# Two states per recurrence instruction, norm constants off GpSimd, and a new order in a two-layer kernel

## The chip, the cores and the metric

The kernel runs on one core of a Trainium2 chip. Times are device microseconds (us); three runs were made, and their median is what is predicted. One more execution was profiled. The engines are called PE (matmuls; PEld is its weight load), DVE (VectorE), ACT (ScalarE), POOL (GpSimd) and SP, whose queue issues the DMAs.

## What is computed

Two layers over x of shape (2, 2048, 256), float32. In each, x becomes x + s(n) * silu(g(n)), where n is x normalised over its 256 columns.

```
layer 0: s = Mamba block, then FFN with gelu(tanh);  g = gated FFN with FP4-quantised inputs and weights
  step:  h = exp(dt_t * A) * h + dt_t * B_t * x_t     # h: (2, 512, 16), one t after the other
         y = sum over the 16 states of h * C_t
layer 1: s = attention over the two batch rows of each token (16 heads)
         g = three blocks: y = qlora(h); y = gelu(layernorm(y)); h = qlora(y) + h
```

The recurrence over t is the one sequential part: 512 channels, 16 states, 2048 steps, two batch rows. Its state starts at zero.

## The kernel before

**Tiles.** The 2048 positions are cut into NJ = 8 blocks of T = 256, for each of the two batch rows: 16 tiles, visited in the order (block, row). A tile passes through stages, one function each: head (line 864: two norms, input projection, convolution, dt, B and C, and ux = dt * xc), fp4_half (1013: quantise, gate and up products, quantise, down), scan (939: the recurrence, and the output projection with its sum x2), tail (1056: norm, FFN, gate, result x1). After both rows of a block, second (1100) does layer 1 for each half g of 128 positions, on streams s0 and s1; for the last block the streams are e0 and e1, which use tiles and PSUM banks that the finished work of layer 0 has left.

**The recurrence** (scan). Channels lie on partitions, in 4 groups m; time runs along the free dimension. For each of the 16 states n: ACT makes decay = exp(dt * A) by four activations into one of two decay tiles; DVE multiplies ux by B into hh; DVE runs a first-order scan over hh, all four groups in one instruction, each group led by one column (decay 0 there, hh the carried state); ACT copies the last columns to the tile state, for the next block; DVE multiplies hh by C, in place; PE transposes and adds the eight 128 x 128 pieces into two PSUM banks y. B and C of two states come by one broadcast DMA (bcs, two buffers). hh has four buffers, decay two; y2, the gated and transposed y, takes a fifth use of the hh buffers.

**Norms.** statistics (695) is DVE's bn_stats and bn_aggr. inverse_root (705) is two POOL instructions on [128, 2]: v * scale + plus, then the power -0.5. normalize (712) has DVE make -mean * root and ACT apply both. head calls inverse_root twice on the same variances. The norms in second's three blocks take the mean out of the weights instead: ACT squares with an accumulated sum, POOL makes the root, ACT scales.

**The order.** No instruction is issued where the code calls it. Recorder (line 32) records every call with its stage; prepare finds the dependences; forward (352) and backward (274) are list schedulers with a cost per instruction (cost, 104, and the tables SEEN and TAIL) that choose the order on each engine and the buffer of each tile; adjust and passes (1256 to 1280) are numbers that shift priorities of stages. issue (548) emits the chosen order, one queue per engine. So every instruction has the line of its emission, L561, in the profile, and is told apart by its tiles. [...]

Of the kernel before, what the change touches and what calls it, by code (L numbers as in the profile page):

```python
# [17 lines left out]
P = 128  # L18
# [23 lines left out]
class Recorder:  # L42
# [14 lines left out]
    TAIL = {"tensor": 0.165, "vector": 0.083, "scalar": 0.1, "gpsimd": 0.8, "sync": 1.7}  # L57
# [46 lines left out]
    def cost(self, engine, method, args, kwargs):  # L104
# [6 lines left out]
        if engine == "gpsimd":  # L111
            if method == "memset":
                return 0.04
            return 0.7 if method == "tensor_tensor" else 0.3
        values = list(args[1:]) + list(kwargs.values())
        tiles = [v for v in values if hasattr(v, "tensor") and v is not out]
        if engine == "tensor":
            rhs = args[2] if len(args) > 2 else kwargs.get("rhs")
            if method == "transpose" or kwargs.get("is_transpose"):
                return 0.109  # L120
            if rhs.dtype == BF16:
                return 0.1 + n / 2400.0
            lhs = kwargs.get("lhsT", args[1] if len(args) > 1 else None)
            if lhs.shape[0] == 16 and lhs.offset >= 16 * lhs.ap[0][0]:
                return 0.1
            return 0.005 + 4 * n / 2400.0
# [6 lines left out]
        if engine == "scalar":  # L133
            inside = bool(tiles) and self.space(tiles[0].tensor) == PSUM
            scalars += kwargs.get("accum_out") is not None
            return (0.05 if inside else 0.093) + 0.000833 * n + 0.1 * scalars
# [12 lines left out]
        if method in ("tensor_copy", "tensor_scalar", "memset") and n >= 64:  # L149
            return 0.07 + 0.00052 * n + 0.06 * scalars  # L150
# [50 lines left out]
    def prepare(self):  # L201
# [12 lines left out]
        for i, (engine, method, args, kwargs, stage) in enumerate(ops):  # L214
            if engine == "tensor":

                n = self.costs[i]
                lhs = kwargs.get("lhsT", args[1] if len(args) > 1 else None)
                if method == "transpose" or kwargs.get("is_transpose"):
                    self.size[i], self.table[i] = 128, 1  # L220
                elif lhs.dtype == BF16:
                    self.size[i], self.table[i] = (n - 0.1) * 2400, 2
                else:
                    self.size[i], self.table[i] = n * 2400 * lhs.shape[0] / 128, 3
            if engine == "sync":
                self.size[i] = 2 if args[0].dtype == BF16 else 4
                for d in args[0].shape:
                    self.size[i] *= d
# [28 lines left out]
    def order(self, lead, bonus, ahead, adjust=(), passes=()):  # L257
# [7 lines left out]
        for unit, bonus_back, ahead_back, bonus, ahead, adjust in passes:  # L265
            key = [-x / unit for x in self.backward(unit, bonus_back, ahead_back)]
            for b, k, v in adjust:
                for i, o in enumerate(self.ops):
                    if o[4] == (b, k):
                        key[i] += v  # L270
# [81 lines left out]
    def forward(self, key, bonus, ahead):  # L352
# [65 lines left out]
        while done < n:  # L418
# [28 lines left out]
            cost = costs[i]  # L447
            if best_e == "scalar" and table[i] and table[i] != now_table:
                t = max(t, free[best_e] + self.SWITCH)
                self.switched += self.SWITCH  # L450
                now_table = table[i]
# [113 lines left out]
def tile_two_layers(ctx: ExitStack, tc: tile.TileContext, a: dict):  # L565
# [25 lines left out]
    def t2k(stream, name):  # L591
        if stream == "e1":
            spare[0] += 1
            return mam.tile([P, 512], F32, tag=("dt", "ux", "lnt")[spare[0] % 3], name=name)
# [8 lines left out]
    power = const.tile([P, TG], F32, name="power")  # L603
    rec.gpsimd.memset(power, -0.5)

# [84 lines left out]
    decay = [const.tile([P, 4, T + 1], F32, tag=f"decay{i}", name=f"decay{i}") for i in range(2)]  # L690
    for t in decay:
        rec.gpsimd.memset(t[:, :, 0], 0.0)
# [12 lines left out]
    def inverse_root(stream, v, n, scale, plus, name):  # L705

        y = small.tile([P, n], F32, tag=f"ln_y_{stream.replace("e", "s")}", name=f"y_{name}")
        rec.gpsimd.tensor_scalar(y, v, scale, plus, ALU.mult, ALU.add)
        rec.gpsimd.tensor_tensor(y, y, power[:, :n], ALU.pow)
# [154 lines left out]
    def head(b, j, xt):  # L864
# [6 lines left out]
        rh = inverse_root("m", mv[:, :, 1], TG, 1.0 + EPS, EPS * EPS, f"a{nm}")  # L871
        normalize("m", xh, xt, TG, mv, rh, f"a{nm}")
        rx = inverse_root("m", mv[:, :, 1], TG, 1.0, EPS, f"x{nm}")
# [50 lines left out]
        ux = mam.tile([P, 4, T], F32, tag="ux", name=f"ux_{nm}")  # L924
        pdt = [bank("m", f"pdt_{nm}_{pr}").rearrange("p (m t) -> p m t", m=2) for pr in range(2)]
# [13 lines left out]
    def scan(b, j, h):  # L939
# [13 lines left out]
        for n in range(NS):  # L953
            if n % 2 == 0:
                bcs = scn.tile([P, 2, 2, T], F32, tag="bcs", name=f"bcs_{nm}_{n}", bufs=2)
                rec.sync.dma_start(bcs, bcv[:, n : n + 2, :].partition_broadcast(P))
            da = decay[n % 2]
            for m in range(4):
                rec.scalar.activation(
                    da[:, m, 1:], dt[:, m, :], AF.Exp, scale=amat[:, m, n : n + 1]  # L960
                )
            hh = scn.tile([P, 4, T + 1], F32, tag="hh", name=f"hh_{nm}_{n}", bufs=4)
            bn = bcs[:, 0, n % 2, :].unsqueeze(1).to_broadcast([P, 4, T])
            cn = bcs[:, 1, n % 2, :].unsqueeze(1).to_broadcast([P, 4, T])

            if j == 0:
                rec.gpsimd.memset(hh[:, :, 0], 0.0)
            else:
                rec.scalar.copy(hh[:, :, 0], state[b][:, n, :])
            rec.vector.tensor_tensor(hh[:, :, 1:], ux, bn, ALU.mult)  # L970
            flat = hh.rearrange("p m t -> p (m t)")
            rec.vector.tensor_tensor_scan(
                flat, da.rearrange("p m t -> p (m t)"), flat, 0.0, ALU.mult, ALU.add
            )
            if j < NJ - 1:
                rec.scalar.copy(state[b][:, n, :], hh[:, :, T])
            rec.vector.tensor_tensor(hh[:, :, 1:], hh[:, :, 1:], cn, ALU.mult)
            for g in range(TG):
                for m in range(4):
                    rec.tensor.matmul(  # L980
                        y[g][:, m * P : (m + 1) * P], lhsT=hh[:, m, 1 + g * P : 1 + (g + 1) * P],
                        rhs=ident, is_transpose=True, start=False, stop=(n == NS - 1),
                        skip_group_check=True,
                    )

        y2 = scn.tile([P, 4, T + 1], F32, tag="hh", name=f"y2_{nm}", bufs=4)[:, :, :T]
        for g in range(TG):
# [12 lines left out]
            rec.scalar.copy(y2[:, :, g * P : (g + 1) * P], pt)  # L1000
        po = bank("m", f"po_{nm}").rearrange("p (g d) -> p g d", g=TG)
        for g in range(TG):
            for m in range(4):
                rec.tensor.matmul(
                    po[:, g, :], lhsT=y2[:, m, g * P : (g + 1) * P],
                    rhs=w_out[:, m, :], start=(m == 0), stop=(m == 3),
                )
        x2 = mam.tile([P, TG, D], F32, tag="x2", name=f"x2_{nm}")
# [91 lines left out]
    def second(j, g, x1):  # L1100
# [3 lines left out]
        xv = x1[:, g, :, :]  # L1104
        xm = t2k(st, f"xm_{nm}").rearrange("p (b d) -> p b d", b=B)
        layer_norm(st, xm, xv, B, f"c{nm}")
# [66 lines left out]
        for k in range(3):  # L1173
# [11 lines left out]
            sq = small.tile([P, B], F32, tag=f"ln_sq_{st.replace("e", "s")}", name=f"sq_{nm}_{k}")  # L1185
            for bb in range(B):
                rec.scalar.activation(
                    yn[:, bb, :], py[:, bb, :], AF.Square, accum_out=sq[:, bb : bb + 1]
                )
            y = inverse_root(st, sq, B, 1.0 / D, EPS, f"f{nm}_{k}")  # L1190
            for bb in range(B):
                rec.scalar.activation(yn[:, bb, :], py[:, bb, :], AF.Copy, scale=y[:, bb : bb + 1])
# [15 lines left out]
            for m in range(2):  # L1208
                rec.scalar.activation(
# [23 lines left out]
    for i, (j, b) in enumerate(order):  # L1233
# [23 lines left out]
        (0, 0, 1.48), (0, 2, 0.93), (0, 3, -0.66), (1, 0, -1.29), (1, 1, -0.08), (1, 3, 0.49),  # L1257
        (1, 4, -0.55), (2, 0, -0.28), (2, 1, 0.62), (2, 4, 0.73), (3, 0, -0.1), (3, 4, 0.51),
        (4, 0, 0.15), (4, 1, 0.67), (4, 2, 0.59), (4, 3, -1.78), (4, 4, -0.74), (5, 0, -0.51),
        (5, 2, 0.63), (5, 3, 0.09), (5, 4, 0.29), (6, 0, 0.66), (6, 1, 1.68), (6, 2, 0.9),  # L1260
        (6, 3, 0.26), (6, 4, 2.72), (7, 0, 0.63), (7, 1, -0.41), (7, 2, 0.3), (7, 4, 0.34),
        (8, 0, -0.58), (8, 1, -0.58), (8, 2, 0.45), (8, 3, 0.6), (8, 4, -0.47), (9, 0, 0.76),
        (9, 1, 2.32), (9, 2, -0.12), (9, 4, -0.53), (10, 0, 0.19), (10, 3, 2.6), (10, 4, 0.12),
        (11, 0, 0.54), (11, 1, -0.16), (11, 2, -0.01), (11, 3, -0.3), (11, 4, 1.13),
        (12, 0, -0.62), (12, 1, 0.85), (12, 2, 0.08), (12, 4, 0.47), (13, 0, 0.34),
        (13, 1, -0.42), (13, 2, -1.48), (13, 4, -0.77), (14, 0, -1.31), (14, 1, 0.5),
        (14, 2, -1.21), (14, 3, -1.46), (14, 4, 0.39), (15, 1, 1.91), (15, 2, -0.55),
        (15, 3, 1.48), (15, 4, 0.61),
# [4 lines left out]
        (110, 0.3, 0.0, 0.5, 0.12, [(9, 0, 0.01)]),  # L1273
        (110, 0.3, 0.1, 0.5, 0.12, [(9, 0, 0.01)]),
        (80, 0.3, 0.0, 0.2, 0.12, []),
        (30, 0.3, 0.05, 0.5, 0.05, []),
        (20, 0.3, 0.1, 0.5, 0.12, []),
        (20, 0.3, 0.1, 0.5, 0.12, [(3, 4, 0.16)]),
    ]
    rec.issue(tc, lead=(0.28, -1.79, 0, -5.22, 1.4), bonus=366.531, ahead=0, adjust=adjust, passes=passes)  # L1280
# [48 lines left out]
```

## Time and profile before

| | us |
|---|---|
| median of three runs (1790.72 to 1791.84) | 1791.33 |
| the profiled execution | 1787.97 |
| its span, first to last instruction | 1786.2 |
| first and last recurrence instruction on DVE (tile hh), from the span's start | 49.9, 1675.1 |
| ACT table loads: 383 of 1283 ns | 491.4 |
| recurrence on DVE: 256 scans, 512 multiplies | 1197.3 |
| state copies on ACT, 448 of about 0.195 | 83.1 |
| POOL: 112 times scale and add, 112 powers | 229.5 |

In a group's row of the profile stand the engine, the operation, out<-in by the program's names, partitions x elements, the count, then the busy time and the mean ns of one, then the idle time of the engine just before and what ended it. "idle <-releaser" names the work whose end let the instruction go. Durations of one engine's neighbours overlap a little: a timeline, which lists start and duration, shows by how much. A float32 matmul of 256 columns stands as two records. The clock that TensorE was granted in the whole span was 0.947.

### The profile page before, as it was taken

The numbers are of one execution on the slowest core, as the hardware profiler recorded it, in microseconds if no ns is written. First come the engines' busy times: TensorE is split into PE (matmuls) and PEld (weight loads), VectorE is DVE, ScalarE is ACT, GpSimd is POOL, SyncE is SP. The second block draws the span as 40 slices with busy tenths as digits, with TensorE's granted clock in tenths as the row PEclk, the third lists the DMA queues.
The fourth block names the chain that finished last, engine by engine and source line by source line (L and its number), as shares of the span: only waits on it lengthen the run. The fifth ranks groups of instructions, "written<-read, shape, count | busy, mean of one in ns | idle before, by whom it ended". The sixth has DMA issues, their size and how long they took to land.

```text
span 1786.2 us, 22221 instructions
## 1 busy us (share of the span) xinstructions
PE 1585.8 (89%) x7756; PEld 1193.1 (67%) x7756; DVE 1630.4 (91%) x1926; ACT 1559.0 (87%) x3324; POOL 233.2 (13%) x265
## 2 busy tenths in 40 slices
PE   7448878999989989899998999999899999998887
PEld 5336656677776768676776767767676767766665
DVE  7999999999989999999998999999998999999711
ACT  7556968899988999989998999999999998999645
POOL 1000010022122201211111021101111102020101
PEclk9669989899999999999999999999999999999989
DMA  6311111111111111212121212211111111212000
GB/s 180 92 41 45 48 43 59 42 45 46 45 48 45 48 49 48 60 36 49 41 61 38 52 43 54 54 31 53 43 60 37 48 49 44 46 36 64 2 6 12
DMA packets 62989, 86.77 MB, mean 49 GB/s; under 512 B 15095, under 2 KB 29085, under 8 KB 62878
## 3 DMA queue, kind: packets, MB, share of 16 engines
q1 hardware_dynamic: 62878, 85.37, 17.9%
q8 instruction: 60, 0.98, 0.2%
q14 instruction: 51, 0.42, 0.1%
HBM read 80.62 MB, written 4.72 MB: 48 GB/s over the span
## 4 chain that ended last, share of the span: by engine, by line
ACT 41%; PE 32%; DVE 19%; issue 5%; POOL 2%; DMA 0%; ACTq 0%; DVEq 0%
ACT L561 14%; PE bank_f L561 13%; ACT decay L561 11%; DVE hh L561 10%; PE bank_m L561 7%; ACT t2k_s L561 6%; PE bank_s L561 5%; PE bank_y L561 4%; DVE fp_l L561 3%; ACT t2k_f L561 3%; PE bank_h L561 2%; POOL ln_y_s L561 2%; ACT xc L561 1%; DVE t2k_s L561 1%; DVE fp_sc L561 1%
## 5 line engine op out<-in xcount | busy, mean ns | idle before, releaser
L561 DVE TENSOR_TENSOR_SCAN hh<-decay,hh 128x1028 f32<-128x1028 f32 x256 | 581.4, 2286 | 5.7 <-ACT decay L561 4.4
L561 ACT ACT_TABLE_LOAD x383 | 491.4, 1283 | 13.9 <-DMA xt<-in_x_dram 3.7
L561 ACT ACTIVATE decay<-dt,amat 128x256 f32<-128x256 f32 x1024 | 445.0, 500 | 6.4 <-DVE hh L561 3.3
L561 PE MATMUL bank_y<-ident,hh 128*128 128x128 f32 x2048 | 296.5, 284 | 30.8 <-DVE hh L561 30.6
L561 DVE TENSOR_TENSOR hh<-hh,bcs 128x1024 f32<-128x1024 f32 x256 | 308.4, 1210 | 15.9 <-ACT state L561 15.2
L561 DVE TENSOR_TENSOR hh<-ux,bcs 128x1024 f32<-128x1024 f32 x256 | 307.5, 1210 | 1.7 <-PE bank_y L561 1.6
L561 PEld LDWEIGHTS bank_y<-ident,hh 128*128 128x128 f32 x2048 | 248.7, 146 | 82.3 <-DVE hh L561 43.1
L561 PE MATMUL bank_f<-w_f,t2k_f 128*128 128x256 f32 x512 | 133.7, 388 | 14.1 <-ACT t2k_f L561 14.0
L561 POOL TENSOR_SCALAR ln_y_s<-ln_sq_s 128x2 f32<-128x2 f32 x48 | 36.9, 769 | 769.8 <-ACT t2k_s L561 458.1
L561 PE MATMUL bank_m<-xi,cdiag 128*128 128x256 f32 x512 | 127.0, 380 | 0.0
L561 PE MATMUL bank_f<-t2k_f,w_f 128*128 128x256 f32 x512 | 124.6, 384 | 2.5 <-ACT t2k_f L561 2.5
L561 PEld LDWEIGHTS bank_f<-w_f,t2k_f 128*128 128x128 f32 x512 | 92.8, 192 | 36.0 <-ACT t2k_f L561 23.5
L561 PE MATMUL bank_f<-w_down,hq 128*128 128x256 f32 (+1 forms) x384 | 103.7, 409 | 7.3 <-ACT hq L561 7.2
L561 PEld LDWEIGHTS bank_f<-t2k_f,w_f 128*128 128x128 f32 x512 | 94.9, 190 | 21.0 <-ACT t2k_f L561 7.1
L561 PE MATMUL bank_h<-t2k_s,w_l 128*128 128x256 f32 x360 | 95.2, 399 | 9.5 <-ACT t2k_s L561 9.2
L561 PEld LDWEIGHTS bank_m<-xi,cdiag 128*128 128x128 f32 x512 | 93.0, 190 | 14.1 <-issue 0.7
L561 DVE SCALAR_TENSOR_TENSOR fp_l<-fp_h,fp_l 128x704 f32<-128x704 f32 (+2 forms) x124 | 91.4, 737 | 7.5 <-ACT fp_h L561 6.9
L561 PE MATMUL bank_f<-ident,fp_l 128*128 128x128 f32 x292 | 54.5, 311 | 47.1 <-DVE fp_l L561 46.5
L561 PE MATMUL bank_f<-w_gate,t2k_f 128*128 128x352 f32 x256 | 92.7, 481 | 2.2 <-ACT h L561 1.1
L561 PEld LDWEIGHTS bank_f<-w_down,hq 128*128 128x128 f32 (+1 forms) x384 | 71.8, 199 | 34.1 <-issue 12.7
L561 POOL TENSOR_TENSOR ln_y_s<-ln_y_s,power 128x2 f32<-128x2 f32 x64 | 93.2, 1457 | 5.2
L561 PE MATMUL bank_f<-w_up,t2k_f 128*128 128x352 f32 x256 | 90.2, 466 | 0.0
(187 smaller groups left out, 2589.9 us busy)
## 6 DMA issues: line engine op xcount, KB each, us to landing
bcs<-bc SPq DMA_DIRECT2D x128, 512.0 KB, 4.8
xt<-in_x_dram SPq DMA_DIRECT2D x16, 256.0 KB, 2.8
out_dram<-t2k_s SPq DMA_DIRECT2D x15, 256.0 KB, 3.8
w_f<-in_ffn_w_dram SPq DMA_DIRECT2D x2, 1024.0 KB
t2k_s<-in_qweights_dram SPq DMA_DIRECT2D x6, 256.0 KB, 2.9
w_in<-in_in_proj_w_dram SPq DMA_DIRECT2D x1, 1024.0 KB
h<-in_w_gate_dram SPq DMA_DIRECT2D x6, 128.0 KB, 2.1
w_qkv<-in_qkv_w_dram SPq DMA_DIRECT2D x1, 768.0 KB
```

Of the source, the lines that this page charges most:

```text
L561: getattr(getattr(self.nc, engine), method)(*args, **kwargs)
```

## The change

It does six things.

- **Two states per call.** hh, decay and the multiplies take two states: [128, 2, 4, 257]. One multiply by B, one scan (2056 elements), one multiply by C, one state copy in and out for a pair. hh has two such buffers, decay two (twice the bytes). The activations and PE's transposes keep their number and size.
- **Room for it.** ux and x2 have one buffer instead of two. y2 is no longer an hh buffer: its two halves take turns on the one buffer t2k_m that head's xh uses too.
- **Norm constants.** v * scale + plus is a DVE instruction now; POOL keeps the power. head makes both constants side by side and one power of four columns. In second's blocks ACT makes it (Identity with scale 1/256 and a bias tile eps).
- **The last block's tiles** (streams e0, e1): normalising is done by DVE (subtract, multiply); the blocks' norms use bn_stats and one DVE multiply instead of ACT's square, sum and scaling; half of hn goes to DVE. The spare tiles of e1 are dt, dt, lnt.
- **The planner**: costs and latencies of POOL, of small matmuls, of accumulating activations and of DVE reading PSUM; a POOL instruction that isn't a memset is planned only where DVE is free; priorities may be shifted for one engine of a stage.
- **adjust, passes, lead, bonus, ahead** are other numbers, so the order on every engine is another.

Counted in the built programs: DVE 1928 to 1650 instructions (branches among them), ACT 3230 to 3006, POOL 270 to 127, PE and SP the same number; ACT table loads 383 to 373.

```diff
@@ Recorder
-    TAIL = {... "gpsimd": 0.8, ...}
+    TAIL = {... "gpsimd": 0.3, ...}
...
+            if best_e == "gpsimd" and table[i]:
+                t = max(t, free["vector"])
@@ inverse_root
-        y = small.tile([P, n], ...)
-        rec.gpsimd.tensor_scalar(y, v, scale, plus, ALU.mult, ALU.add)
-        rec.gpsimd.tensor_tensor(y, y, power[:, :n], ALU.pow)
+        m = 2 * n if and_also else n
+        y = small.tile([P, m], ...)
+        rec.vector.tensor_scalar(y[:, :n], v, scale, plus, ALU.mult, ALU.add)
+        if and_also:
+            rec.vector.tensor_scalar(y[:, n:], v, *and_also, ALU.mult, ALU.add)
+        rec.gpsimd.tensor_tensor(y, y, power[:, :m], ALU.pow)
@@ head
-        ux = mam.tile([P, 4, T], F32, tag="ux", name=f"ux_{nm}")
+        ux = mam.tile([P, 4, T], F32, tag="ux", name=f"ux_{nm}", bufs=1)
@@ scan
-        for n in range(NS):
-            if n % 2 == 0:
-                bcs = ...; rec.sync.dma_start(bcs, ...)
-            da = decay[n % 2]
-            for m in range(4):
-                rec.scalar.activation(da[:, m, 1:], dt[:, m, :], AF.Exp, scale=amat[:, m, n : n + 1])
-            hh = scn.tile([P, 4, T + 1], F32, tag="hh", name=f"hh_{nm}_{n}", bufs=4)
+        for n in range(0, NS, 2):
+            bcs = ...; rec.sync.dma_start(bcs, ...)
+            da = decay[n // 2 % 2]
+            for k in range(2):
+                for m in range(4):
+                    rec.scalar.activation(
+                        da[:, k, m, 1:], dt[:, m, :], AF.Exp, scale=amat[:, m, n + k : n + k + 1]
+                    )
+            hh = scn.tile([P, 2, 4, T + 1], F32, tag="hh", name=f"hh_{nm}_{n}", bufs=2)
...
-                rec.scalar.copy(hh[:, :, 0], state[b][:, n, :])
-            rec.vector.tensor_tensor(hh[:, :, 1:], ux, bn, ALU.mult)
-            flat = hh.rearrange("p m t -> p (m t)")
+                rec.scalar.copy(hh[:, :, :, 0], state[b][:, n : n + 2, :])
+            rec.vector.tensor_tensor(hh[:, :, :, 1:], un, bn, ALU.mult)
+            flat = hh.rearrange("p k m t -> p (k m t)")
...
-                rec.scalar.copy(state[b][:, n, :], hh[:, :, T])
-            rec.vector.tensor_tensor(hh[:, :, 1:], hh[:, :, 1:], cn, ALU.mult)
+                rec.scalar.copy(state[b][:, n : n + 2, :], hh[:, :, :, T])
+            rec.vector.tensor_tensor(hh[:, :, :, 1:], hh[:, :, :, 1:], cn, ALU.mult)
...
-        y2 = scn.tile([P, 4, T + 1], F32, tag="hh", name=f"y2_{nm}", bufs=4)[:, :, :T]
+            y2[g] = t2k("m", f"y2_{nm}_{g}").rearrange("p (m t) -> p m t", m=4)
...
-        x2 = mam.tile([P, TG, D], F32, tag="x2", name=f"x2_{nm}")
+        x2 = mam.tile([P, TG, D], F32, tag="x2", name=f"x2_{nm}", bufs=1)
@@ second
+        last = st[0] == "e"
...
+            if last:
+                mv = statistics(st, py, B, f"f{nm}_{k}")
+                y = inverse_root(st, mv[:, :, 1], B, 1.0, EPS, f"f{nm}_{k}")
+                rec.vector.tensor_tensor(yn, py, y.unsqueeze(2).to_broadcast([P, B, D]), ALU.mult)
+            else:
...
+                rec.scalar.activation(sq, sq, AF.Identity, scale=1.0 / D, bias=eps)
+                rec.gpsimd.tensor_tensor(y, y, power[:, :B], ALU.pow)
...
+                if last and m == 1 and k < 2:
+                    rec.vector.tensor_scalar(hn[:, m, :], hb[:, m, :], wt["odd"][:, k, m : m + 1], None, ALU.add)
+                    continue
@@ adjust, passes, issue
-    rec.issue(tc, lead=(0.28, -1.79, 0, -5.22, 1.4), bonus=366.531, ahead=0, ...)
+    rec.issue(tc, lead=(12.22, -6.26, 0, -7.42, 1.15), bonus=193.318, ahead=0.034, ...)
```

## The prediction

> **What bounds the kernel now.** I read the page's first part, then busy time by stretch, then VectorE's waits, then the groups, then timelines.
>
> The first part shows three engines near 90%, so it decides nothing:
>
> ```profile
> PE 1585.8 (89%) x7756; PEld 1193.1 (67%) x7756; DVE 1630.4 (91%) x1926; ACT 1559.0 (87%) x3324; POOL 233.2 (13%) x265
> ```
>
> I cut the span at VectorE's first and last recurrence instruction (those on tile hh), at 49.9 and 1675.1 us. Columns: stretch, length, busy us (instructions) of PE, PEld, DVE, ACT, POOL, then clock, DMA.
>
> ```profile
> 0.00:49.90 49.90, 39.56 (x180) 29.30 (x181) 35.90 (x121) 35.88 (x70) 8.88 (x25) 1.00 0.69 178
> 49.90:1675.10 1625.20, 1452.79 (x7173) 1097.07 (x7173) 1569.92 (x1750) 1463.53 (x3123) 213.65 (x218) 0.95 0.18 47
> 1675.10:1786.20 111.10, 93.47 (x407) 66.72 (x405) 24.59 (x57) 59.57 (x132) 10.67 (x23) 0.93 0.02 8
> ```
>
> In the middle DVE works 1569.9 of 1625.2 us and is idle 55.3: it is the bound there. In the last 111 us it is nearly empty: a chain PE-ACT-DVE-POOL sets that end. DVE's longest waits in the middle:
>
> ```profile
> DVE hh L561 <- ACT state L561: 15.2, 14, 3.5
> DVE sz L561 <- PE bank_y L561: 7.4, 6, 4.3
> DVE hh L561 <- ACT decay L561: 4.4, 6, 1.8
> ```
>
> The groups, and DVE's timeline for what one instruction really occupies:
>
> ```profile
> L561 DVE TENSOR_TENSOR_SCAN hh<-decay,hh 128x1028 f32<-128x1028 f32 x256 | 581.4, 2286 | 5.7 <-ACT decay L561 4.4
> L561 DVE TENSOR_TENSOR hh<-hh,bcs 128x1024 f32<-128x1024 f32 x256 | 308.4, 1210 | 15.9 <-ACT state L561 15.2
> L561 DVE TENSOR_TENSOR hh<-ux,bcs 128x1024 f32<-128x1024 f32 x256 | 307.5, 1210 | 1.7 <-PE bank_y L561 1.6
> ```
>
> ```profile
> 905.63 1.22 DVE L561 TENSOR_TENSOR hh<-hh,bcs 128x1024 f32<-128x1024 f32 x1
> 906.77 1.22 DVE L561 TENSOR_TENSOR hh<-ux,bcs 128x1024 f32<-128x1024 f32 x1
> 907.91 0.68 DVE L561 TENSOR_TENSOR fp_l<-fp_l,fp_sc 128x512 f32<-128x512 f32 x1
> 908.51 1.22 DVE L561 TENSOR_TENSOR hh<-ux,bcs 128x1024 f32<-128x1024 f32 x1
> ```
>
> A multiply lasts 1.22 us but the next starts 1.14 us on; the 512-element one takes 0.60. So an element costs (1.14-0.60)/512 = 1.05 ns and the instruction 0.06 to 0.07 us. Two scans take 4.41 us from start to next start in the same timeline (898.91 to 903.32): 2.205 each, of which 1028 elements at twice that rate leave again some 0.065.
>
> **The change, middle stretch.**
>
> *Pairs.* 768 recurrence instructions become 384 of double length: 384 fixed parts go, 384 x 0.067 = **-25.7 us**. [...] I take 25.7. No row shows a multiply over two states with both operands broadcast; if the longer pattern streams no faster than two instructions do, the gain is 0; if not even that, the kernel loses; the nearest rows scale by elements, so I keep the full gain.
>
> *Constants of the norms.* 70 two-element DVE instructions replace GpSimd ones, 55 of them in the middle. The nearest row (ln_m, two elements) lasts 0.146; in the timeline two take 0.22 with the second's tail, so 0.075 each: **+4.1**. The 42 of the LoRA norms go to ACT instead, 0.1 each on an engine that doesn't bound.
>
> *Moved by the new order.* I counted the built orders. Before the first hh instruction stand 148 DVE instructions instead of 122 (two more weight blocks quantised, one more LoRA weight, less one ux): **-5.4** from the middle. After the last stand 121 instead of 57; of the work that was in the middle, one quantisation of 704 columns (4.4), the two gate products (0.9), one attention mix (2.6) and a gate by s (1.2) are now behind: **-9.1**.
>
> Sum: 1569.9-25.7+4.1-5.4-9.1 = 1533.8 of work. Idle 55.3 kept: **1589**, against 1625.
>
> Does the idle stay? For it: decay now holds four states instead of two, so ACT may run further ahead; state copies fall by 224 (0.08 us from start to start at 920.03, so 18 us of ACT), table loads from 383 to 373 (1.30 each: 13). Against it: hh holds the same bytes in two pieces, not four. In the orders, DVE has 3.4 us of other work on average between a scan and the multiply by C, which waits for ACT's state copy; in the new one 2.6. And ux, x2 have one buffer, y2 shares one. The ux product now has to stand between the last multiply by B of one tile and the first of the next; all three are on DVE, and only ACT's dt can be late (0.2 us now): 0, at worst 1 us in each of 14 tiles. The second y2 copy waits for four matmuls on the first, about 1.7 us; PE has other work (bank_f, bank_s); 0, at worst 16 x 1.7. I take 55, and 30 to 85 for the range.
>
> *GpSimd.* One instruction per norm instead of two. Power takes longest beside DVE:
>
> ```profile
> L561 POOL TENSOR_TENSOR ln_y_s<-ln_y_s,power 128x2 f32<-128x2 f32 x64 | 93.2, 1457 | 5.2
> 1673.03 3.06 POOL L561 TENSOR_TENSOR ln_y_s<-ln_y_s,power 128x2 f32<-128x2 f32 x1
> 1741.99 0.69 POOL L561 TENSOR_TENSOR ln_y_s<-ln_y_s,power 128x2 f32<-128x2 f32 x1
> ```
>
> 0.69 beside an idle DVE, 3.06 beside a busy one. [...] by the row that hardly matters, since DVE waits for GpSimd only 2.4 us in the whole middle, ACT 13.1. As one of two such waits goes, I take 0, and +3 for the range.
>
> **First stretch.** x is now the eleventh DMA on SP's queue instead of the first: 7 small issues of 0.3 and 3 of 0.5 us ahead, +4 us for the first head. But the bias rows' DMAs, which held the queue from 30.9 to 34.5 and the broadcast of B and C behind them, stand earlier. DVE's 36+5 us of work fit. I take **50**, unchanged (46 to 55).
>
> **End stretch**, by its landmarks in the timelines: last hh ends 1675.1; x2 at 1691.1; the FFN's sum 1714.0; second's transposed input 1725.0; end 1786.2.
> - x2: in the new order all of the last quantisation and eight gate/up products stand ahead of it on DVE. A 256-column matmul takes 0.44 us (the chain has 56 records, two each, in 12.41 us). 11.4 us of DVE work, transposes and copy 1.1, six w_down 2.7, eight of 352 columns 4.9, Silu and product 1.1, quantisation with its trip to ACT 6: 27 instead of 16, **+11**.
> - FFN: 11 more matmuls of the previous tile interleaved on PE, 0.44 each: **+5**.
> - second's norm: before, ln_m waited behind two other DVE instructions until 1721.7, then ACT made four halves in 2.1 us. Now four DVE instructions of 0.2 follow the power directly: **-4**.
> - three blocks per tile: the squares took ACT 0.84, statistics take DVE 0.97; GpSimd 0.96 becomes 0.69; scaling 0.82 becomes 0.69; the two halves of hn run side by side, 0.84 to 0.47. Some 0.7 to 1 each, **-3**. ACT no longer serves both tiles in turn, and the second tile, which ends last and lagged by 10 us (1731.5 against 1741.2), has its q, k, v ahead of the first one's output product: **-4**.
>
> 111+5 = **116** (106 to 124).
>
> **Sum.** 50+1589+116 = 1755 of span; 1.8 lie around it (1787.97-1786.2), and the median of the runs is 3.4 above that execution: **1760**.
>
> **Rivals.**
> 1. As worked out, 1760: 0.62.
> 2. The deeper decay buffers and the lighter ACT take half of DVE's idle: 1760-28 = 1732. For: 19.6 of the 55 us are waits for state and decay. Against: no engine gets slack, PE's work is unchanged. 0.16.
> 3. The end gives the gain back: +16 for its longer chain and none of the 11 saved: 1771; with y2's wait uncovered half the time (+13), 1784. 0.14.
> 4. Slower: the multiply by C stalls in place. In the new order 50 of 128 scans have under 1.5 us of other DVE work before it (40 of 256 before). ACT's queue puts a table load and an activation, 1.3+0.5, ahead of the copy. If each of these lost one load, 50 x 1.28 = 64, less the 15 paid now: +49, 1809. It decides from 0.6 us per tight pair on. Against: the last tiles need no copy, and loads became fewer. 0.05.
> 5. The pair instructions stream slower than by elements: at 2% more, +22, 1782; 0.03.
>
> A measurement can tell 0.2%, 3.6 us, from no change. Faster (below 1787.7): 0.62+0.16+0.12+0.02 = 0.92; within: 0.03; slower: 0.05. The range takes in idle of 30 (1735) and, upward, rival 3's 1784.
>
> **What would show it.** Scan near 4.43 us and multiply near 2.28 by duration, or the pairs are priced wrong. DVE busy 1530 to 1540 between first and last hh, idle near 55; if "DVE hh <- ACT state" exceeds 40, rival 4 acts. ux, x2, y2 must not appear as long waits. x2 some 27 us after the last hh. Wrong if PE, whose matmuls it doesn't change, turns out to hold the middle at 1625: then DVE's idle would simply grow by 36.

## The result and the profile after

The changed kernel took 1790.03 us (median of 20 runs, 1783.87 to 1792.72), the kernel before 1791.12 on the same chips (20 runs): a ratio of 1.0000, 95% interval 0.9987 to 1.0012. The prediction, 1760, is missed by 30 us; the time did not change. The profiled execution of the changed kernel took 1792.72, its span is 1790.5. It lies 2.7 us above its median, the profiled one of the kernel before 3.2 below its own: differences of a few us between the two profiles mean nothing.

The first part of the page:

```profile
PE 1591.0 (89%) x7756; PEld 1206.1 (67%) x7756; DVE 1622.9 (91%) x1648; ACT 1519.2 (85%) x3088; POOL 164.2 (9%) x122
```

Busy time by stretch, cut as before at the first and last hh instruction of DVE (now 63.5 and 1668.9):

```profile
0.00:63.50 63.50, 45.62 (x167) 32.83 (x168) 42.51 (x147) 32.44 (x70) 4.16 (x15) 0.87 0.61 161
63.50:1668.90 1605.40, 1440.32 (x7110) 1097.48 (x7110) 1532.21 (x1382) 1428.94 (x2910) 151.50 (x95) 0.95 0.18 47
1668.90:1790.50 121.60, 105.02 (x482) 75.80 (x480) 48.19 (x120) 57.81 (x109) 8.52 (x12) 0.99 0.02 7
```

DVE's work in the middle is 1532.2 us; 1533.8 was predicted. What was not predicted is its idle time: 73.2 instead of 55. The middle is 1605.4 (predicted 1589), the first stretch 63.5 (50), the end 121.6 (116). Against the kernel before, the middle became 19.8 us shorter, but the first stretch 13.6 longer and the end 10.5.

DVE's longest waits in the middle:

```profile
DVE hh L567 <- ACT state L567: 19.2, 26, 3.8
DVE hh L567 <- PE bank_y L567: 14.7, 7, 5.0
DVE h L567 <- PE bank_f L567: 11.2, 10, 3.3
```

The second and third stood at 1.6 and 2.0 before. The groups of the recurrence:

```profile
L567 DVE TENSOR_TENSOR_SCAN hh<-decay,hh 128x2056 f32<-128x2056 f32 x128 | 567.0, 4429 | 1.5 <-ACT hh L567 0.7
L567 DVE TENSOR_TENSOR hh<-hh,bcs 128x2048 f32<-128x2048 f32 x128 | 291.6, 2280 | 19.7 <-ACT state L567 19.2
L567 DVE TENSOR_TENSOR hh<-ux,bcs 128x2048 f32<-128x2048 f32 x128 | 291.5, 2277 | 14.9 <-PE bank_y L567 14.7
```

Scan 4.43 and multiply 2.28, as priced; two single ones took 2 x 2.286 and 2 x 1.210 before.

The prediction left out part 4 of the page, the chain that ended last. It goes back from the last instruction, at each step to what released it or to the instruction before it on its engine, and gives each engine's share of the span. Before:

```profile
ACT 41%; PE 32%; DVE 19%; issue 5%; POOL 2%; DMA 0%; ACTq 0%; DVEq 0%
```

After:

```profile
PE 41%; ACT 40%; DVE 13%; issue 5%; POOL 1%; DMA 0%; ACTq 0%; DVEq 0%
```

DVE, busiest of all in the middle, stood on a fifth of the chain before the change. The two kernels' progress agrees in the long run, though their orders differ everywhere. Starts of the multiply by B of some pairs, in us:

| pair (of 128) | 1st | 5th | 17th | 73rd | 113th | last |
|---|---|---|---|---|---|---|
| before | 49.9 | 106.3 | 251.0 | 959.2 | 1476.1 | 1665.1 |
| after | 63.5 | 108.0 | 251.7 | 958.7 | 1476.4 | 1657.7 |

Between these pairs they differ more, either way: at the 13th the changed kernel is 10.1 us behind, at the 22nd 10.2, at the 42nd 20.0 ahead, at the 103rd 15.7 behind. Over pairs 5 to 128 it is 1.2 us behind on average. So the late start is made up by about the 33rd pair, and after that little is gained before the last tile. This suggests that something that the change left alone sets the pace.

### The profile page after: what moved, and what is told of

Read it like the earlier page. It is cut to its first block, busy times and chain, and to the rows that moved or that the text cites. A ratio compares the mean times of both kernels' runs of the same rounds, so it can differ in the third digit from the quotient of the medians.

```text
span 1790.5 us, 21456 instructions
## 1 busy us (share of the span) xinstructions
PE 1591.0 (89%) x7756; PEld 1206.1 (67%) x7756; DVE 1622.9 (91%) x1648; ACT 1519.2 (85%) x3088; POOL 164.2 (9%) x122
## 4 chain that ended last, share of the span: by engine, by line
PE 41%; ACT 40%; DVE 13%; issue 5%; POOL 1%; DMA 0%; ACTq 0%; DVEq 0%
PE bank_f L567 15%; ACT L567 14%; ACT decay L567 11%; PE bank_m L567 10%; DVE hh L567 8%; PE bank_s L567 7%; PE bank_y L567 6%; ACT t2k_s L567 5%; PE bank_h L567 3%; DVE fp_l L567 3%; ACT t2k_f L567 3%; ACT xc L567 1%; ACT dt L567 1%; POOL ln_sq_s L567 1%; ACT fp_h L567 1%
## 5 line engine op out<-in xcount | busy, mean ns | idle before, releaser
L567 DVE TENSOR_TENSOR_SCAN hh<-decay,hh 128x2056 f32<-128x2056 f32 x128 | 567.0, 4429 | 1.5 <-ACT hh L567 0.7
L567 ACT ACT_TABLE_LOAD x373 | 478.6, 1283 | 15.2 <-PE bank_h L567 4.1
L567 PE MATMUL bank_y<-ident,hh 128*128 128x128 f32 x2048 | 283.2, 286 | 31.2 <-DVE hh L567 31.2
L567 DVE TENSOR_TENSOR hh<-hh,bcs 128x2048 f32<-128x2048 f32 x128 | 291.6, 2280 | 19.7 <-ACT state L567 19.2
L567 DVE TENSOR_TENSOR hh<-ux,bcs 128x2048 f32<-128x2048 f32 x128 | 291.5, 2277 | 14.9 <-PE bank_y L567 14.7
L567 PE MATMUL bank_f<-w_f,t2k_f 128*128 128x256 f32 x512 | 134.0, 392 | 17.0 <-ACT t2k_f L567 16.9
L567 POOL TENSOR_TENSOR ln_sq_s<-ln_sq_s,power 128x2 f32<-128x2 f32 x42 | 74.4, 1771 | 742.7 <-ACT ln_sq_s L567 742.7
L567 PE MATMUL bank_f<-w_up,t2k_f 128*128 128x352 f32 x256 | 91.2, 473 | 10.1 <-ACT h L567 6.4
L567 PE MATMUL bank_f<-w_gate,t2k_f 128*128 128x352 f32 x256 | 91.9, 480 | 2.7 <-ACT h L567 1.9
L567 PE MATMUL bank_s<-w_l,t2k_s 128*128 128x256 f32 x336 | 87.0, 395 | 7.4 <-ACT t2k_s L567 7.3
```

The lines of the kernel that those rows point to most:

```text
L567: getattr(getattr(self.nc, engine), method)(*args, **kwargs)
```

## The experiments

My theory after the result: ScalarE's and TensorE's queues pace the middle, and time taken from DVE turns into idle time. Its first rival: DVE does pace it, and the pairs' coarser pieces cost as much by waits as they save. All kernels but three (order_free, free_state, and bcs_early, which moves two DMAs) keep the planned order of the kernel that they start from and change instructions only where issue emits them; of(v) is the name of v's tile. Measured, all in one table (each ratio is to the kernel before on the same chip; the last column is (ratio - 1) x 1791):

| run | median us | ratio, 95% interval | us |
|---|---|---|---|
| (the change itself) | 1790.03 | 1.0000, 0.9987 to 1.0012 | 0 |
| split | 1788.51 | 0.9990, 0.9979 to 1.0001 | -2 |
| dve_pad | 1786.81 | 0.9966, 0.9952 to 0.9979 | -6 |
| dve_cut | 1785.71 | 0.9954, 0.9940 to 0.9968 | -8 |
| before_cut | 1771.90 | 0.9903, 0.9876 to 0.9930 | -17 |
| half_transposes | 1796.18 | 1.0032, 1.0020 to 1.0045 | +6 |
| pe_pad | 1804.97 | 1.0083, 1.0055 to 1.0112 | +15 |
| act_pad | 1811.88 | 1.0115, 1.0085 to 1.0146 | +21 |
| act_half | 1768.87 | 0.9864, 0.9839 to 0.9890 | -24 |
| pe_act_cut | 1758.73 | 0.9794, 0.9771 to 0.9816 | -37 |
| rest_cut | 1733.45 | 0.9683, 0.9658 to 0.9709 | -57 |
| no_power | 1780.64 | 0.9931, 0.9910 to 0.9952 | -12 |
| shift_c | 1797.75 | 1.0041, 1.0027 to 1.0055 | +7 |
| bcs_early | 1792.05 | 1.0003, 0.9992 to 1.0014 | +1 |
| order_free | 1785.07 | 0.9941, 0.9922 to 0.9959 | -11 |
| state_dve | 1774.06 | 0.9876, 0.9856 to 0.9897 | -22 |
| more_dve | 1788.49 | 0.9970, 0.9948 to 0.9992 | -5 |
| free_state | 1775.99 | 0.9905, 0.9890 to 0.9920 | -17 |
| before_state | 1804.63 | 1.0070, 1.0056 to 1.0083 | +12 |

**Is VectorE the bound?** Four kernels: the pairs undone, VectorE loaded, and relieved, after and before the change.

split:

```diff
+    if engine == "vector" and of(args[0]) == "hh":
+        for k in range(2):      # half k of every operand
+            cut = slice(k * 4 * (T + 1), (k + 1) * 4 * (T + 1)) if method == "tensor_tensor_scan" else k
+            emit(engine, method, [v[:, cut] for v in operands])
```

> The changed kernel's order kept instruction for instruction, but each of the 384 recurrence instructions over two states issued as two over one state, back to back. Theory A (VectorE sets the middle and the pairs save their fixed parts): 384 x 0.067 = 25.7 us more, about 1816, the idle time of VectorE between first and last hh stays near 73. Theory B (the middle is held by other engines and queues, the saved time turns into idle): the split is absorbed, 1790 to 1800, and VectorE's idle falls to about 50.

The middle of split (stretch, length, busy us of PE, PEld, DVE, ACT, POOL):

```profile
61.30:1663.60 1602.30, 1438.87 (x7109) 1092.43 (x7108) 1551.79 (x1766) 1429.66 (x2910) 126.13 (x95) 0.95 0.18 47
```

DVE works 19.6 us more than in the changed kernel, and the middle is 3.1 shorter: idle 50.5 instead of 73.2. That is theory B of that text. So the pairs' saving is real work saved (for a multiply 0.068 per pair: two single ones follow each other at 1.135, a pair at 2.202), and undoing it cost no time. But the shorter pieces also helped others: in the middle the powers on GpSimd took 124.5 us instead of 149.9, and TensorE's idle time before the matmuls into y, until hh was ready, fell from 31.2 to 20.2. So this result alone would also fit the rival, VectorE's cost hidden by waits saved.

dve_pad:

```diff
+    if engine == "vector" and of(args[0]) == "hh":
+        nc.vector.memset(spare, 0.0)      # spare: [128, 16]
```

> The changed kernel's order kept, and behind each of the 384 recurrence instructions a memset of 16 columns on VectorE, some 0.065 us each: the same 25 us of VectorE's time that the split cost, without its shorter pieces. Theory A (VectorE is only 13% of the chain that ended last, ScalarE and TensorE hold the middle): 3 to 6 us more, 1793 to 1796. Theory B (VectorE does set the middle, and the split was free because its shorter pieces release TensorE and ScalarE earlier): 20 us more or over, 1810.

Not more but 6 us less. As a load it failed: the memsets, 384 of 0.072 us, lie mostly in the tail of the instruction before (one starts at 1121.39, where the multiply before it ends at 1121.44), and DVE's busy time in the middle grew by only 6.4. So it cannot decide against theory B. A place where it gained stands below, at GpSimd.

dve_cut, and before_cut with the same edit on the kernel before:

```diff
+    if engine == "vector" and method == "tensor_tensor" and of(args[1]) == "hh":
+        seen += 1
+        if seen % 2: continue
```

> The changed kernel's order kept, but the multiply by C is left out for every second pair (64 x 2.20 = 141 us of VectorE less); the output is then not the reference's. Theory A (VectorE does not set the middle): 13% of it, some 18 us, 1765 to 1785. Theory B (VectorE sets it): 70 us less or more, until the next engine holds at about 1720.

> The kernel before with its own order, but the multiply by C left out for every second state (128 x 1.14 = 146 us of VectorE less); the output is not the reference's. Theory A (VectorE did not set the middle before the change either, 19% of the chain): 10 to 28 us less than the kernel before, 1763 to 1781. Theory B (it did, and only the changed order moved the bound): 60 us less or more, 1730.

The middle of dve_cut, then of before_cut:

```profile
62.50:1658.30 1595.80, 1437.77 (x7102) 1097.14 (x7101) 1397.54 (x1318) 1428.40 (x2909) 140.13 (x95) 0.94 0.19 47
50.00:1656.00 1606.00, 1443.63 (x7167) 1092.39 (x7166) 1436.66 (x1622) 1460.92 (x3122) 186.58 (x218) 0.95 0.18 48
```

DVE has 134.7 us less to do and the middle loses 9.6; DVE is idle for 198 us. In before_cut 133 us less give 17. The outcome is nearest theory A both times (dve_cut even gained less than the 18 us named there): a us taken from DVE was worth 0.13 before the change, where the chain gave it 19%, and 0.06 after it. This refutes the first half of the rival: if DVE paced, the cuts would have shown it. That the coarser pieces cost something by waits is not refuted; split's waits say that they do, and how much is open.

**What paces the middle?** Loads and cuts on the other two.

act_pad and pe_pad:

```diff
+    if args[2] == AF.Exp and args[0].shape[-1] == T:  # act_pad
+        exps += 1
+        if exps % 4 == 0: nc.scalar.copy(spare, power)      # four elements
...
+    if engine == "tensor" and method == "transpose":  # pe_pad
+        turns += 1
+        if turns % 4 == 0: nc.tensor.transpose(*args, **kwargs)      # once more
```

> The changed kernel's order kept, and behind every fourth decay exponential a copy of four elements on ScalarE: 256 x 0.09 = 23 us more of ScalarE's time. Theory A (TensorE sets the pace; leaving out 226 us of ScalarE's work took only 21 off): 2 to 6 us more. Theory B (ScalarE, with 40% of the chain that ended last, sets it as much as TensorE): 10 us more or over.

> The changed kernel's order kept, and every fourth plain transpose issued twice: 217 more matmuls of about 0.11 us, 24 us more of TensorE's time, nothing else changed. Theory A (TensorE's queue sets the pace of the middle): 15 to 25 us more, 1805 to 1815. Theory B (no single engine does, each has slack of its own): under 8 us more.

The middle of act_pad, then of pe_pad:

```profile
64.10:1687.30 1623.20, 1442.53 (x7109) 1093.58 (x7108) 1533.20 (x1382) 1451.10 (x3162) 152.37 (x95) 0.95 0.18 47
64.50:1683.80 1619.30, 1455.65 (x7300) 1116.91 (x7299) 1532.89 (x1382) 1432.18 (x2910) 156.49 (x95) 0.95 0.18 47
```

22 us more of ScalarE make the middle 18 longer and the time 21: 0.9 us for each. TensorE's 19 us more in the whole span (15.3 in the middle) cost 15: 0.8 for each, theory A at its lower end. ScalarE's outcome is theory B of its text: a load on it is paid as much as one on TensorE. On VectorE split's 19.6 us cost nothing. What speaks against waits saved by shorter pieces as the reason is state_dve below: it adds 17 us to VectorE with the pairs whole and gains 22; had the 17 been paid in full, the 19 us taken off ScalarE would have to be worth twice their size. It does not settle it, as that move also ends VectorE's waits for the copies (19.2 us).

act_half and half_transposes, and pe_act_cut with both edits:

```diff
+    if args[2] == AF.Exp and args[0].offset >= 4 * (T + 1):  # act_half: the pair's second state
+        exps += 1
+        if exps > 8: continue
...
+    if engine == "tensor" and of(kwargs["lhsT"]) == "hh" and not kwargs["stop"]:  # half_transposes
+        if kwargs["lhsT"].offset >= 4 * (T + 1): continue
```

> The changed kernel's order kept, but 504 of the 1024 decay exponentials of the recurrence are left out (with 15 table loads some 226 us of ScalarE less); the output is then not the reference's. Theory A (ScalarE's queue, 40% of the chain that ended last, holds the middle): the time falls until VectorE's 1532 us of work hold it, by 40 or more, 1750 or less. Theory B (ScalarE waits for others as much as they for it): 1780 to 1790.

> The changed kernel's order kept, but TensorE leaves out the transposes (and sums into y) of every second state but the last, about 960 matmuls of 0.17 us, 160 us of its work; the output is then not the reference's. Theory A (VectorE sets the middle): what can go is its waits for TensorE, some 30 us, so 1760 to 1775. Theory B (TensorE with its 90% is the real bound of the middle): nearly all of VectorE's idle goes, 60 us or more, 1730 or less. If the clock is held back because TensorE has less to do, its granted clock in the middle falls under 0.95, and less is gained by both.

> The changed kernel's order kept, with both cuts that did nothing or little alone: 896 transposes into y and 504 decay exponentials left out; the output is not the reference's. Theory A (TensorE and ScalarE pace the middle in turn): much more than the 0 and 21 us of the single cuts, 1745 or less. Theory B (something else is left, or TensorE's clock falls as its work does): 1765 to 1770, as with the exponentials alone.

The middle of half_transposes, then of act_half:

```profile
64.00:1671.20 1607.20, 1374.49 (x6213) 1002.45 (x6211) 1531.60 (x1382) 1428.15 (x2909) 152.47 (x95) 0.93 0.18 47
64.00:1646.50 1582.50, 1423.26 (x7117) 1096.05 (x7115) 1529.70 (x1383) 1224.83 (x2391) 151.95 (x95) 0.96 0.19 48
```

With 896 transposes left out their group falls from 283.2 us to 174.0, by 109, but TensorE's busy time in the middle by 66 only: other matmuls took longer (the 512 of bank_f<-w_f 138.6 us instead of 134.0, the 256 of bank_f<-w_gate 96.1 instead of 91.9). The granted clock went from 0.95 to 0.93, by estimate 29 us (1374.5 x 0.02/0.95); the rest may lie in the ends of matmuls, which the profile models. Neither theory's number came: it is 6 us slower. Longer matmuls on the chain may be the cause, but no run shows it. So a load on TensorE is paid, while this relief brought nothing. act_half lies between its two theories as well: 204 us less on ScalarE gave 24. The middle of pe_act_cut, whose 37 us lie between its two theories (13 more than act_half alone):

```profile
63.80:1634.80 1571.00, 1355.54 (x6230) 997.82 (x6228) 1528.99 (x1383) 1224.37 (x2391) 150.45 (x95) 0.94 0.18 48
```

Now DVE is busy for 97% of it. That it has become the bound is likely but not shown, as it was busy for 96.6% of the middle before the change too. So a load on ScalarE or TensorE is paid at 0.8 to 0.9, and a large relief is worth far less: 0.12 for each of act_half's 204 us.

rest_cut has the edits of act_half, dve_cut and no_power together.

> The changed kernel's order kept, with 504 decay exponentials, every second multiply by C and all powers of the norms left out together (ScalarE 226, VectorE 141, GpSimd 150 us less); the output is not the reference's. TensorE's work is untouched. Theory A (TensorE's 1591 us of work are the floor): the three cuts still leave 1700 or more, and TensorE's busy share of the middle goes to 93% or over. Theory B (the slack of the engines adds up, none sets the pace): the savings of the single cuts, 4, 21 and 10 us, are far surpassed, 1690 or less.

57 us, more than the 44 of its single cuts (24, 8 and 12), and TensorE's share of the middle rose to 1408.6 of 1546.8, 91%, not 93. Theory A holds by its time. The page followed the chain through 69% of the span: TensorE has 48%, VectorE 10 and ScalarE 9.

**GpSimd's powers.** no_power:

```diff
+    if engine == "gpsimd" and method == "tensor_tensor":
+        method, args = "memset", (args[0], 1.0)
```

> The changed kernel's order kept, but GpSimd's power in every norm is replaced by a memset of ones, so that the norms' scales are left out and the output is not the reference's. Theory A (powers held back behind VectorE's long instructions stand on the chain that ended last, which gives GpSimd 1 to 2%): 15 to 30 us less, 1760 to 1775. Theory B (their delay is covered): 1786 to 1790.

12 us less (1780.64 lies between the two theories): the powers do stand on the chain. How much of the 12 is the 0.69 us of the shortest ones and how much what others last beyond it, this run does not part. Here is the longest, on GpSimd's timeline (start, us) of the changed kernel:

```profile
1127.58 10.16 POOL L567 TENSOR_TENSOR ln_sq_s<-ln_sq_s,power 128x2 f32<-128x2 f32 x1 [45.13 <-ACT ln_sq_s L567]
```

and DVE beside it:

```profile
1127.82 2.28 DVE L567 TENSOR_TENSOR hh<-hh,bcs 128x2048 f32<-128x2048 f32 x1
1130.02 2.28 DVE L567 TENSOR_TENSOR hh<-ux,bcs 128x2048 f32<-128x2048 f32 x1
1132.22 0.68 DVE L567 TENSOR_TENSOR fp_l<-fp_l,fp_sc 128x512 f32<-128x512 f32 x1
1132.82 4.43 DVE L567 TENSOR_TENSOR_SCAN hh<-decay,hh 128x2056 f32<-128x2056 f32 x1
```

The power ends at 1137.74, 0.5 us after DVE's run of these four back-to-back instructions, which ends at 1137.2. In dve_pad the same power stands ahead of the same four instructions:

```profile
1128.22 0.95 POOL L572 TENSOR_TENSOR ln_sq_s<-ln_sq_s,power 128x2 f32<-128x2 f32 x1 [45.12 <-ACT ln_sq_s L572]
```

dve_pad gains on the changed kernel in its profile just here: it is 0.6 us behind at the 85th pair and 5.1 ahead at the 89th; no_power gains 5.7 between the same two. Whether the memset just ahead of it (at 1127.96) let it in, or that it came 0.32 us before the multiply instead of 0.24, the runs do not tell.

shift_c makes the multiply by C write one column to the left, so that ScalarE's copy of the last column does not hold it:

```diff
+    if engine == "vector" and method == "tensor_tensor" and of(args[1]) == "hh":
+        args = (left(args[0]), *args[1:])      # offset - 1
+    if engine == "tensor" and of(kwargs["lhsT"]) == "hh":
+        kwargs["lhsT"] = left(kwargs["lhsT"])
```

> The changed kernel's order kept, but the multiply by C writes its result one column to the left, so that the last column of each state stays and ScalarE's copy of it no longer holds the multiply; TensorE's transposes read one column to the left as well. Theory A (the waits for the copy, 19.2 us in 26 places, are time of the bound engine): 1771 to 1775. Theory B (the next wait, for TensorE or the next instruction's input, takes their place): 1785 to 1790.

The copy's wait, 19.2 us in the changed kernel, is gone from DVE's longest, and the kernel is 7 us slower, beyond both theories. Up to the 101st pair it is 3.3 ahead, four pairs later 4.2 behind, and between them stands

```profile
1320.88 9.85 POOL L578 TENSOR_TENSOR ln_sq_s<-ln_sq_s,power 128x2 f32<-128x2 f32 x1 [17.58 <-ACT ln_sq_s L578]
```

a power that took 2.56 in the changed kernel: there it stood from 1323.81 to 1326.37, beside a multiply that ended at 1325.82. Why it took 9.85 here, the runs do not tell, and that this is all of the loss was not tried alone.

**The late start.** bcs_early puts the first two broadcasts of B and C ahead of four LoRA loads on SP's queue:

```diff
+    late = first two dma_start into bcs
+    order = order without late; order[at:at] = late      # at: the next load of lora_a behind the DMAs into bc
```

> The changed kernel's order kept, only the first two broadcasts of B and C moved ahead of four LoRA loads on SP's queue, of which the first waits 6.2 us for its buffer. Theory A (the late start is this wait in an in-order queue): first multiply by B near 55 instead of 63.5, and the whole time 8 lower, 1782. Theory B (the start is late because the first head and TensorE's half clock are late, or the transfer is slow among others): first multiply at 61 or later, time within 2 of 1790. Theory C: the start moves by 8, but the middle gives it back as idle time: first multiply 55, time 1787 to 1791.

SP's queue in the changed kernel, where the loads come first:

```profile
52.92 0.33 SPq L567 DMA_DIRECT2D t2k_s<-in_lora_a_dram  x1
...
53.82 0.90 SPq L567 DMA_DIRECT2D bcs<-bc  x2
```

and in bcs_early:

```profile
45.44 0.89 SPq L579 DMA_DIRECT2D bcs<-bc  x2
51.65 0.34 SPq L579 DMA_DIRECT2D t2k_s<-in_lora_a_dram  x1
```

The broadcasts went out 8.4 us earlier, and the first multiply came 1.2 earlier:

```profile
58.72 0.42 DVE L579 SCALAR_TENSOR_TENSOR fp_l<-fp_h,fp_l 128x256 f32<-128x256 f32 x1 [5.42 <-ACT fp_h L579]
...
62.34 2.28 DVE L579 TENSOR_TENSOR hh<-ux,bcs 128x2048 f32<-128x2048 f32 x1
```

It stands in DVE's queue behind this quantisation, which waits 5.42 us for ScalarE; in the changed kernel ScalarE waits 3.86 us of this stretch for TensorE. Theory B. The broadcast was late, but not last.

**The order itself.** order_free takes six numbers from the last ordering pass:

```diff
-        (20, 0.5, 0.1, 0.5, 0.08, [(1, 0, 'scalar', 0.478), (13, 1, 'gpsimd', -0.64), ...]),
+        (20, 0.5, 0.1, 0.5, 0.08, []),
```

> The changed kernel with the six hand-set numbers of its last ordering pass taken out, nothing else; about a sixth of the instructions stand elsewhere on their engines. Theory A (the pace comes from the work on ScalarE and TensorE, the exact order matters little): 1785 to 1800. Theory B (the time owes much to the particular order): over 1800.

11 us less than the kernel before, at the lower end of theory A. One other order is no distribution; it does show that the order that came with the change is not the best for its code.

**Moving work to the engine that is free.** If ScalarE is paid at 0.9 and VectorE at nothing, the copies of the states belong on VectorE. state_dve, and more_dve with one name more:

```diff
+    if engine == "scalar" and method == "copy" and (of(args[0]) == "hh" or of(args[1]) == "hh"):
+        engine, method = "vector", "tensor_copy"
...
+    ... of(args[0]) in ("hh", "xi") ...      # more_dve
```

> The changed kernel's order kept, but the 224 small copies of the states (out of hh and into it) go from ScalarE to VectorE: 224 x 0.084 = 19 us less on ScalarE, 224 x 0.075 = 17 us more on VectorE. Theory A (ScalarE and TensorE pace the middle, VectorE's time is free): 1772 to 1786, the price of ScalarE's time being 1.0 for small steps and 0.1 for large ones. Theory B (VectorE is as near the bound as they are): 1790 or more.

> As the kernel with the states' copies on VectorE, and the 32 copies of xi out of PSUM go there too: another 32 x 0.55 = 18 us from ScalarE to VectorE. Theory A: again 2 to 10 us less than that kernel. Theory B (at some 1655 us of work VectorE becomes the bound): more than that kernel by 5 or over.

The middle and the chain of state_dve:

```profile
63.60:1651.90 1588.30, 1431.98 (x7111) 1093.61 (x7111) 1549.08 (x1606) 1409.90 (x2686) 143.72 (x95) 0.95 0.19 48
```

```profile
PE 39%; DVE 29%; ACT 23%; issue 9%; POOL 1%; DMA 0%; ACTq 0%; DVEq 0%; POOLq 0%
```

19 us moved, 22 gained: faster than both kernels, by 1.24% than the one before. The chain shows the price: ScalarE from 40 to 23%, VectorE from 13 to 29. The next step is already too far. more_dve loads VectorE with 16 us more in the middle, leaves it idle for 35 of 1599.8, and gives 17 us back (theory B). free_state joins state_dve and order_free:

> The changed kernel without the six hand-set numbers of its last ordering pass, and the state copies on VectorE. Theory A (the two gains, 16 us by the copies and 5 by the order, are of different kinds and add up): 1766 to 1772. Theory B (both take away the same waits): 1773 to 1780.

1775.99, no better than state_dve: the gains do not add up (theory B).

before_state makes the move on the kernel before. There y2 is an hh tile too, so the condition also took its 32 copies out of PSUM (0.58 each on ScalarE), which was not meant:

> The kernel before with its own order, but its 448 small copies of the states (out of hh and into it) on VectorE instead of ScalarE: 448 x 0.084 = 38 us less on ScalarE, some 448 x 0.075 = 34 us more on VectorE. Theory A (ScalarE paced the middle before the change too, and VectorE's idle time, 55 us, takes the 34): 1765 to 1780. Theory B (VectorE, at 96.6% of the middle, was as near the bound): 1787 or more.

DVE got 49 us more and was busy for 1618.9 of 1642.6. With 55 us of idle time it did not carry that: 12 us slower, theory B. The intended 34 us alone were not tried. So it is likely, but not shown, that state_dve lives on the room that the pairs made on VectorE.

## Why the prediction was wrong

**The step that failed** is the first: "In the middle DVE works 1569.9 of 1625.2 us and is idle 55.3: it is the bound there", and with it "Idle 55.3 kept". A high share of busy time says that an engine has little room, not that the others wait for it. What the runs showed in its place: DVE's idle time grew to 73.2; 133 us taken off it in the kernel before gave 17, and 135 in the changed one 8; some 20 us more on ScalarE or TensorE cost 21 and 15. ScalarE and TensorE, at 90 and 89% of the middle, were what most of DVE's gaps waited for (31.0 and 15.5 of the 55.3 us). The page's chain gave DVE 19%: by estimate 25.7 x 0.19 = 5 us for the pairs instead of 25.7. The case named at the end of the prediction, that TensorE holds the middle and DVE's idle grows by 36, came half true: idle grew by 18, and a load on ScalarE is paid as much.

**The prices.** DVE's work in the middle was right in sum, 1533.8 against 1532.2, but in part by luck: by split the pairs save 19.6 us of it, not 25.7, so the other terms, not measured one by one, took off some 8 us more than booked. The pairs were mis-sized by the scans. Two single scans of split start 2.191 apart where they follow each other, a pair 4.351: 0.031 saved, half of the 0.067 taken. (By the prediction's own rate, 2.205 - 1028 x 0.0021 leaves 0.046, not 0.065.) For a multiply split shows 0.068, against 0.067 taken. In the two cuts each us taken off DVE was worth 0.06 to 0.13, not 1.

**ScalarE's 40 us** (1559.0 to 1519.2), booked as an argument that the idle stays, have no single price. At act_half's 0.12 they would be worth some 5 us; at the rate of state_dve, whose 19 us gained 22, some 40. With DVE's 38 us at 0.06 to 0.13 the change's savings come to 7 to 10 us by the low price. Not even these are in the time. order_free's 11 us and the powers' 12 are large enough to hold the low sum, not the high one. What took the savings back stays open. One candidate is the new order itself: the pairs with the order numbers of the kernel before were not run.

**GpSimd** was taken at 0, with 3 for the range. In the middle the 81 powers took 149.9 us, the 95 of the kernel before 130.9, and the longest 10.16 instead of 7.14; against that, the scale and add beside each is gone from GpSimd. (The prediction's row of 0.69 at 1741.99 had no idle VectorE beside it: a reduction ran there from 1742.02 to 1742.71. The 0.69 at 1702.84 had.) Leaving the powers out gains 12 in the changed kernel; as this was not tried before the change, what the change added to it is open.

**First stretch**: 63.5, not 50 (46 to 55). I allowed 4 us for x standing eleventh on SP's queue; ux of the first tile started at 40.3 instead of 30.0, and from 40 to 56 us TensorE's granted clock was 0.50. It was made up within the first quarter of the pairs.

**End stretch**: 121.6 against 116. x2 came 28.3 us after the last hh (27 predicted), the FFN's sum 29.7 after that (28), and from there to the end 63.6 (61, against 72.3 before). So of the 11 us booked as saved there 8.7 came; which of the three savings brought them was not measured.

**The rivals.** The second, that DVE's idle time shrinks, went the other way. The fourth, a stall of the multiply by C, did not come (19.2 us of wait instead of 15.2), nor the fifth. The third had a part: the end took 10.5 us.

## What to carry to other kernels

Where several engines are busy for 85 to 97% of a stage, ask the chain of waits, not the busy share, which of them is paid, and test it with a small load on each: here some 20 us cost 21 on ScalarE, 15 on TensorE and nothing on VectorE (there with shorter pieces). Large cuts tell less: they gave 0.06 to 0.13 for each us on VectorE and ScalarE, and nothing on TensorE. Time saved on an engine that is not paid is room: worth little until work is moved into it from one that is, and only as much as fits: here 19 us moved gained 22, and 16 more gave 17 back. Where every instruction has a planned place, another order of the same work can be worth as much as the edit under test.

## What the runs showed that I had not expected

- A GpSimd power that takes 0.69 us at its shortest lasted 10.16 beside a run of four VectorE instructions, until 0.5 us after their end; in dve_pad, started ahead of the same four, it took 0.95. Another took 9.85 in shift_c and 2.56 in the changed kernel.
- 16-column memsets behind long VectorE instructions cost almost nothing: 384 of 0.072 us, 27.6 in sum, added 6.4 us of busy time.
- Leaving out 896 transposes lowered TensorE's granted clock in the middle twice: from 0.95 to 0.93 (half_transposes), and from 0.96 in act_half to 0.94 in pe_act_cut.
- A table load on ScalarE takes 1.28 us, 373 of them 478.6 us: more than a quarter of the span and the largest single item on the engine that is paid most. No run here took any away by itself.
